# Attention over two key blocks at a time: both score products, then the values of the two blocks before, across pair and group borders, with two sum banks

## The chip, the core and the metric

The kernel runs on one core of a Trainium2 chip. The metric is the device time in microseconds of one execution. The core has TensorE (PE, the matrix engine, which writes to PSUM only), VectorE (DVE), ScalarE (ACT), GpSimd (POOL) and SyncE (SP, which here issues the DMAs of images and results). Each engine works through its own list of instructions in order and waits for other engines by semaphores. PSUM has eight banks.

## The reference, cut to what matters

The input is four images of 384 channels on a 48 x 48 grid, 2304 tokens each, float32. Eight heads of 48 channels:

```
local  = batchnorm(depthwise 7x7 conv of x)                  # per channel
q,k,v  = layernorm(x) @ qkv_w.T + qkv_b                      # per token
q      = q + layernorm(local)
attn   = softmax(q @ k.T / sqrt(48));  out = attn @ v        # per head, 2304 x 2304
result = x + out @ proj_w.T + proj_b
```

## The kernel before

Everything is in `attention_pass`, called once with `shifted=False`; a second call under a condition (with maxima subtracted) doesn't run on these inputs. An image's 2304 queries are cut into 6 groups (g) of 384, the heads into 4 pairs (p), and the keys into 18 blocks (kb) of 128. For each image, group and pair, `attention` goes over the 18 key blocks:

- **scores** (L435): for both heads of the pair, 48 rows each at partitions 0 and 64, keys times queries into a PSUM tile `s` of two banks (pool `ps_s`, two such tiles, four banks in all);
- **exponentials** (L443): one ScalarE instruction over both heads, into `pt`;
- **values** (L421): `pt` of the block before times its values, with a column of ones that sums the weights, added up over the 18 blocks in one PSUM bank `o` (pool `ps_o`, one bank). The two heads take partitions 0 to 48 and 64 to 112.

After the last block ScalarE (L454) and VectorE (L455) copy the two halves of `o` to `osb`, and the next pair may use the bank.

All other work is cut into small steps by Python generators in a queue `behind`; `advance(units)` runs three steps after each key block, `finish` all that are left. The steps are:

- `kv_part(b, g)`: normalize the tokens, project keys and values;
- `q_part(b, g)`: the 49 taps of the convolution for each of three channel blocks (L265, L269, VectorE, into one buffer `acc`), its transposes to tokens and normalization (`lt`), the normalization of the tokens themselves, and per pair a projection (L206), a transpose of `lt` (L287) and the sum of both (L292), which is the query;
- `pair_output` (L342 to L354): three transposes of `osb` on TensorE, then the division on VectorE into `ao`;
- `group_output` (L368 to L385): three transposes of `ao` to a PSUM bank each, copied to `aoT`, then the output projection (L378), the residual sum (L385), and the DMA out.

`normalized` (L142) turns three blocks of tokens by transposes (L152), copies them out (ACT, L153), takes mean and variance (DVE, L156 and L157), raises to -1/2 on GpSimd (L159, L160) and normalizes (DVE, L164); `x_normalized` turns the result back (L190, L193). All these, the projections and the output use one PSUM pool, `ps_m`, of three banks with the tag `m`.

The query work of group g + 1 is queued at pair 0 of group g; before pair 3 `finish` runs what is left of it. A pair's output is appended at the queue's end after its last block.

The order on each engine isn't that of the source: the tile framework schedules when the program is built and moves instructions of independent work past each other on each engine, within what the buffers allow. So steps such as the taps, which need no PSUM, are moved far ahead.

## Time and profile before

| | us |
|---|---|
| median of 3 runs (4406.0 to 4411.12) | 4408.76 |
| the profiled execution | 4405.68 |
| its span, from the first to the last instruction | 4403.8 |
| ACT busy on exponentials (L443) | 1388.8 |
| DVE busy on taps (L269) | 1870.4 |
| PE rows of the scores (L435) | 1725.5 |
| PE rows of the values (L421) | 1510.4 |

A row of the profile names a line, an engine, an operation and its tiles; "x4" is the number of instructions merged into it. In a timeline the first figure is the start within the span, the second the time from the first instruction's start to the last one's end, and a bracket at the end holds the idle time ahead and who ended it. PE's rows overlap a little, since a matmul's end is modelled: starts are the safer figures. The clock is the share of TensorE's full speed that was granted. Here are the slices of the whole span, in tenths:

```profile
PE   6899999999899989999989999999998999999998
DVE  7674835735634484484372547546528174664510
ACT  2344343444334434434433443443443344344444
PEclk9889988999899989999989998999998999899999
```

PE is busy nearly everywhere, with dips at the same place in each image; DVE's share swings between the stretches with taps and those without.

### The profile page before, as it was taken

Reading aid. Unit: us, or ns where it says so; the run is one execution under the profiler, and the core shown is the slowest. Engines: PE = TensorE matmul, PEld = TensorE weight load, DVE = VectorE, ACT = ScalarE, POOL = GpSimd, SP = SyncE. Lnnn points to the kernel's source line nnn. Section 1 sums busy time; section 2 is a strip of 40 time slices with the busy share of each in tenths; the row PEclk is TensorE's granted clock in tenths of the full one; section 3 lists DMA queues with packets and bytes.
Section 4 is the critical chain, followed back from the end, with each engine's and each line's share of the span. In section 5 each row is a group of like instructions: output and inputs, shape, how many; then the busy total and the mean of one; then the engine's idle time right before and its main releaser. Section 6 shows DMA issues by size and latency. Waiting matters only on the chain.

```text
span 4403.8 us, 45704 instructions
## 1 busy us (share of the span) xinstructions
PE 4059.2 (92%) x17714; PEld 1551.7 (35%) x17714; DVE 2339.0 (53%) x4908; ACT 1760.3 (40%) x2449; POOL 182.1 (4%) x325
## 2 busy tenths in 40 slices
PE   6899999999899989999989999999998999999998
PEld 3433332333353333333344333333334433233332
DVE  7674835735634484484372547546528174664510
ACT  2344343444334434434433443443443344344444
POOL 1000000000000000000000000000000000000000
PEclk9889988999899989999989998999998999899999
DMA  2000000000000000000000000000000000000000
GB/s 57 0 1 6 6 1 6 6 33 6 6 1 1 6 6 1 6 6 33 6 6 1 1 6 6 1 6 6 36 2 6 1 6 1 6 6 1 6 6 7
DMA packets 20420, 33.99 MB, mean 8 GB/s; under 512 B 8416, under 2 KB 18656, under 8 KB 18656
## 3 DMA queue, kind: packets, MB, share of 16 engines
q1 hardware_dynamic: 12096, 28.32, 1.7%
q10 hardware_dynamic: 8096, 2.65, 0.3%
q8 instruction: 141, 2.31, 0.2%
q14 instruction: 87, 0.71, 0.1%
HBM read 16.80 MB, written 14.16 MB: 7 GB/s over the span
## 4 chain that ended last, share of the span: by engine, by line
PE 65%; DVE 29%; POOL 3%; ACT 2%; issue 1%; DMA 0%; ACTq 0%; POOLq 0%
DVE acc L269 23%; PE s L435 23%; PE o L421 21%; PE pm L206 10%; PE pm L378 3%; PE pm L228 3%; PE pm L190 2%; DVE st L156 2%; POOL rs L160 1%; PE pm L368 1%; PE pm L152 1%; ACT pt L443 1%; DVE osb L455 1%; PE pm L287 1%; DVE lt L164 1%
## 5 line engine op out<-in xcount | busy, mean ns | idle before, releaser
L443 ACT ACTIVATE pt<-s 128x768 f32<-128x768 f32 x1728 | 1388.8, 810 | 1546.4 <-PE s L435 1505.7
L269 DVE SCALAR_TENSOR_TENSOR acc<-x,cw,acc 128x368 f32<-128x368 f32 (+10 forms) x3456 | 1870.4, 588 | 36.5
L435 PE MATMUL s<-q,k 48*128 48x384 f32 x6912 | 1725.5, 546 | 5.7 <-ACT pt L443 5.7
L421 PE MATMUL o<-pt,v 128*49 128x384 f32 x6912 | 1510.4, 517 | 49.7 <-DVE osb L455 36.3
L435 PEld LDWEIGHTS s<-q,k 48*128 48x128 f32 x6912 | 583.0, 189 | 1070.6 <-issue 1018.2
L421 PEld LDWEIGHTS o<-pt,v 128*49 128x49 f32 x6912 | 310.1, 124 | 984.3 <-issue 887.6
L455 DVE COPY osb<-o 49x384 f32<-49x384 f32 x96 | 53.8, 560 | 939.0 <-ACT osb L454 937.5
L206 PE MATMUL pm<-xnT,w_qk 128*128 128x384 f32 x1152 | 454.0, 546 | 2.9 <-ACT xnT L193 2.9
L156 DVE BATCH_NORM_STATS2 st<-xt 128x6 f32<-128x384 f32 x216 | 112.4, 547 | 609.8 <-ACT xt L153 609.1
L206 PEld LDWEIGHTS pm<-xnT,w_qk 128*128 128x128 f32 x1152 | 236.6, 215 | 182.8 <-issue 41.8
L190 PE MATMUL pm<-ident,xt 128*128 128x128 f32 x432 | 98.5, 381 | 144.0 <-DVE xt L164 142.9
L378 PE MATMUL pm<-aoT,w_o 128*128 128x384 f32 x432 | 170.0, 546 | 0.0
L153 ACT COPY xt<-pm 128x384 f32<-128x384 f32 x216 | 93.2, 484 | 181.9 <-PE pm L152 181.8
L342 PE MATMUL pm<-ident,osb 113*128 113x113 f32 x288 | 54.0, 303 | 119.1 <-DVE osb L455 115.9
L193 ACT ACTIVATE xnT<-pm,ln_sb 128x384 f32<-128x384 f32 x144 | 88.0, 668 | 185.9 <-PE pm L190 185.9
L213 ACT ACTIVATE q<-pm,qkb 128x384 f32<-128x384 f32 x96 | 55.7, 581 | 227.5 <-PE pm L206 227.5
L228 PE MATMUL pm<-w_v,xnT 128*128 128x384 f32 x432 | 144.0, 487 | 0.0
L235 DVE TENSOR_TENSOR v<-pm,vb 128x384 f32<-128x384 f32 x72 | 40.0, 555 | 183.0 <-PE pm L228 183.0
L190 PEld LDWEIGHTS pm<-ident,xt 128*128 128x128 f32 x432 | 70.3, 191 | 185.1 <-DVE xt L164 103.0
L159 POOL TENSOR_SCALAR rs<-mv 128x3 f32<-128x3 f32 x72 | 28.6, 397 | 2569.3 <-DVE mv L157 2569.3
L378 PEld LDWEIGHTS pm<-aoT,w_o 128*128 128x128 f32 x432 | 90.5, 219 | 68.8 <-issue 31.9
L213 ACT ACTIVATE k<-pm,qkb 128x384 f32<-128x384 f32 x96 | 55.7, 580 | 142.0 <-PE pm L206 142.0
(52 smaller groups left out, 1057.0 us busy)
## 6 DMA issues: line engine op xcount, KB each, us to landing
x<-in_x_dram SPq DMA_DIRECT2D x12, 1152.0 KB, 7.5
out_dram<-xr SPq DMA_DIRECT2D x72, 192.0 KB, 1.8
w_qk<-in_qkv_wT_dram ACTq DMA_DIRECT2D x6, 192.0 KB, 5.1
w_v<-in_qkv_wT_dram ACTq DMA_DIRECT2D x3, 192.0 KB, 5.4
w_o<-in_proj_wT_dram ACTq DMA_DIRECT2D x3, 192.0 KB, 3.9
vb<-in_v_b_dram ACTq DMA_DIRECT2D x1, 192.0 KB, 4.4
cw<-in_conv_w_dram ACTq DMA_DIRECT2D x1, 73.5 KB, 5.9
ln_p<-in_ln_pair_dram ACTq DMA_DIRECT2D x2, 1.5 KB, 5.2
```

The lines of the kernel that those rows point to most:

```text
L153: nc.scalar.copy(xt[:, blk, :], tp[:, :C])
L156: nc.vector.bn_stats(st[:, blk, :], xt[:, blk, :])
L190: nc.tensor.transpose(tp[:, blk * P : (blk + 1) * P], kept["xn"][:, blk, c * P : (c + 1) * P], ident)
L206: nc.tensor.matmul(ps[:, :G], lhsT=w_qk[:, c, which, 2 * p : 2 * p + 2, :].rearrange("p h d -> p (h d)"), rhs=xnT[:, c, :], start=c == 0, ...
L213: nc.scalar.activation(dst, ps[:, :G], AF.Identity, bias=qkb[:, which, p : p + 1])
L228: nc.tensor.matmul(ps[:, :C], lhsT=xnT[:, c, blk * P : (blk + 1) * P], rhs=w_v[:, c, :], start=c == 0, stop=c == CC - 1,)
L269: nc.vector.scalar_tensor_tensor(dst, src, cw[:, c, t : t + 1], dst, ALU.mult, ALU.add)
L378: nc.tensor.matmul(ps[:, :G], lhsT=w_o[:, c, co * P : (co + 1) * P], rhs=aoT[:, c, :], start=c == 0, stop=c == CC - 1,)
L421: nc.tensor.matmul(o[r : r + HA, :G], lhsT=values[b, kb // NB][:, kb % NB, 2 * p + j, :], rhs=pt[:, j, :], start=kb == 0, stop=kb == KB - 1,)
L435: nc.tensor.matmul(s[:, j, :G], lhsT=keys[b, kb // NB][r : r + HS, p, blk * P : (blk + 1) * P], rhs=q[r : r + HS, :], start=True, stop=True,)
L443: nc.scalar.activation(pt, s[:, :, :G], AF.Exp, scale=SCALE)
L455: nc.vector.tensor_copy(osb[64 : 64 + HA, :], o[64 : 64 + HA, :G])
```

## The change

Blocks are handled in batches of `BATCH = 2`. A batch issues both score products and both exponentials, and then the values of the batch before, also when that belongs to the pair before or to the group before: the closure that does it is kept in the list `weighing`. The copies of the sums to `osb` follow the last values of a pair, wherever these come, and the pair's division is handed on in `divisions`, to be put at the head of the queue `behind` at the next batch, ahead of the taps. The sums get two banks and the other work two in place of three; `pt` gets four buffers in place of three; the six steps of two blocks run at once after a batch. `finish` moves, for this pass, from pair 3 to pair 0. At the end of an image the last values, divisions and output are issued before the key and value parts of the next.

```diff
-    ps_o = ctx.enter_context(tc.tile_pool(name="ps_o", bufs=1, ...PSUM))
-    ps_m = ctx.enter_context(tc.tile_pool(name="ps_m", bufs=3, ...PSUM))
+    ps_o = ctx.enter_context(tc.tile_pool(name="ps_o", bufs=2, ...PSUM))
+    ps_m = ctx.enter_context(tc.tile_pool(name="ps_m", bufs=2, ...PSUM))
...
+    weighing = []
+    divisions = deque()
+    def weigh_last():
+        if weighing:
+            weighing.pop()()
...
+        def weigh(batch):
+            for kb, pt in batch:
+                for j in range(2):
+                    r = 64 * j
+                    nc.tensor.matmul(o[r : r + HA, :G], ...)
+            if batch[-1][0] == KB - 1:
+                nc.scalar.copy(osb[0:HA, :], o[0:HA, :G])
+                nc.vector.tensor_copy(osb[64 : 64 + HA, :], o[64 : 64 + HA, :G])
+                divisions.append((b, g, p, osb))
+        for k0 in range(0, KB, BATCH):
+            while divisions:
+                done = divisions.popleft()
+                if done[2] == NP - 1:
+                    behind.appendleft(group_output(*done[:2]))
+                behind.appendleft(pair_output(*done))
+            batch = []
+            for kb in range(k0, k0 + BATCH):
...
+                pt = work.tile([P, 2, G], F32, tag="pt", name="pt", bufs=2 * BATCH)
+                nc.scalar.activation(pt, s[:, :, :G], AF.Exp, scale=SCALE)
+                batch.append((kb, pt))
+            weigh_last()
+            weighing.append(lambda batch=batch: weigh(batch))
...
+            advance(BATCH * units)
...
-                if p == NP - 1 and g < NG - 1:
+                if p == (NP - 1 if shifted else 0):
                     finish()
...
+        weigh_last()
+        while divisions:
+            behind.append(pair_output(*divisions.popleft()))
+        behind.append(group_output(b, NG - 1))
```

How the built program's order moves is shown at three places, all in the first image. The lines of the changed kernel are 1 to 20 higher. Names: `q_2_3` is the query tile of group 2, pair 3; `k_5` and `v_5` are keys and values of group 5; "x2" counts matmuls of one head each.

**TensorE, the border from group 2, pair 3 to group 3, pair 0.** Before:

```order
L421 MATMUL o<-pt,v_4_526 49x384 x2
L435 MATMUL s<-q_2_3_2440,k_5_609 128x384 x2
L421 MATMUL o<-pt,v_5_610 49x384 x2
L435 MATMUL s<-q_2_3_2440,k_5_609 128x384 x2
L421 MATMUL o<-pt,v_5_610 49x384 x2
L435 MATMUL s<-q_3_0_3274,k_0_189 128x384
L421 MATMUL o<-pt,v_5_610 49x384 x2
L435 MATMUL s<-q_3_0_3274,k_0_189 128x384 x3
L342 MATMUL pm<-ident,osb 128x113 x3
L368 MATMUL pm<-ident,ao 128x128 x6
```

Now:

```order
L455 MATMUL s<-q_2_3_2537,k_5_609 128x384 x4
L431 MATMUL o<-pt,v_4_526 49x384 x2
L431 MATMUL o<-pt,v_5_610 49x384 x2
L455 MATMUL s<-q_3_0_3357,k_0_189 128x384 x4
L431 MATMUL o<-pt,v_5_610 49x384 x4
L455 MATMUL s<-q_3_0_3357,k_0_189 128x384 x2
L455 MATMUL s<-q_3_0_3357,k_1_273 128x384 x2
L431 MATMUL o<-pt,v_0_190 49x384 x4
L343 MATMUL pm<-ident,osb 128x113 x3
L369 MATMUL pm<-ident,ao 128x128 x3
L455 MATMUL s<-q_3_0_3357,k_1_273 128x384
L369 MATMUL pm<-ident,ao 128x128 x3
```

Scores and values now stand in runs of four where they alternated in runs of two, the last values of the old pair stand behind the first scores of the new one, and the transposes of `osb` come after one more batch.

**TensorE, the normalization of the next tokens around pair 3 of group 2** (`x_83` is the image, `xt` its turned and normalized tokens). Before:

```order
L152 MATMUL pm<-ident,x_83 128x128 x2
L421 MATMUL o<-pt,v_5_610 49x384 x2
L152 MATMUL pm<-ident,x_83 128x128 x7
L435 MATMUL s<-q_2_3_2440,k_0_189 128x384 x6
L190 MATMUL pm<-ident,xt 128x128 x9
L435 MATMUL s<-q_2_3_2440,k_1_273 128x384
```

Now:

```order
L343 MATMUL pm<-ident,osb 128x113 x3
L153 MATMUL pm<-ident,x_83 128x128 x3
L455 MATMUL s<-q_2_3_2537,k_1_273 128x384
L153 MATMUL pm<-ident,x_83 128x128 x3
L455 MATMUL s<-q_2_3_2537,k_1_273 128x384 x3
L431 MATMUL o<-pt,v_0_190 49x384 x2
L431 MATMUL o<-pt,v_1_274 49x384 x2
L191 MATMUL pm<-ident,xt 128x128 x2
L455 MATMUL s<-q_2_3_2537,k_2_357 128x384
L191 MATMUL pm<-ident,xt 128x128
L455 MATMUL s<-q_2_3_2537,k_2_357 128x384 x3
L431 MATMUL o<-pt,v_1_274 49x384 x4
```

Between the last transpose in and the first one out stood three score blocks; now there stand one and a half score blocks and two value blocks, and the transposes of `osb` come just ahead.

**VectorE, the copy of the sums at the border from group 2 to group 3** (`acc` is written by a tap, `ao` by the division). Before, with 58 taps ahead of the copy back to the last of a division:

```order
L269 SCALAR_TENSOR_TENSOR acc<-x_83,cw,acc 128x8x47 x2
L455 COPY osb<-o 49x384
L269 SCALAR_TENSOR_TENSOR acc<-x_83,cw,acc 128x384
L269 SCALAR_TENSOR_TENSOR acc<-x_83,cw,acc 128x8x46
L348 RECIPROCAL rden<-pm 128x6
L269 SCALAR_TENSOR_TENSOR acc<-x_83,cw,acc 128x8x47
L353 SCALAR_TENSOR_TENSOR inside<-rden,inside 128x6
L354 TENSOR_TENSOR ao<-pm,rden 128x3x96
```

Now, with 37 taps ahead of it back to the last query:

```order
L270 SCALAR_TENSOR_TENSOR acc<-x_83,cw,acc 128x384
L440 COPY osb<-o 49x384
L270 SCALAR_TENSOR_TENSOR acc<-x_83,cw,acc 128x8x47
L270 SCALAR_TENSOR_TENSOR acc<-x_83,cw,acc 128x8x46 x2
L270 SCALAR_TENSOR_TENSOR acc<-x_83,cw,acc 128x8x45 x3
L349 RECIPROCAL rden<-pm 128x6
L270 SCALAR_TENSOR_TENSOR acc<-x_83,cw,acc 128x8x46
L354 SCALAR_TENSOR_TENSOR inside<-rden,inside 128x6
L355 TENSOR_TENSOR ao<-pm,rden 128x3x96
```

The copy still stands behind a long run of taps, a shorter one, and six taps in place of two lie between it and the division.

More of the change, by code (lines that the diff above doesn't have):

```diff
@@ L20 @@
 BN_EPS = 1e-5
+BATCH = 2
 RG = 8
@@ new lines, in attention @@
+        for k0 in range(0, KB, BATCH):
[6 more added lines that the diff above has]
+            for kb in range(k0, k0 + BATCH):
+                s = ps_s.tile([P, 2, 512], F32, tag="s", name="s")
+                blk = kb % NB
+                for j in range(2):
+                    r = 64 * j
+                    nc.tensor.matmul(
+                        s[:, j, :G],
+                        lhsT=keys[b, kb // NB][r : r + HS, p, blk * P : (blk + 1) * P],
+                        rhs=q[r : r + HS, :],
+                        start=True,
+                        stop=True,
+                    )
+                pt = work.tile([P, 2, G], F32, tag="pt", name="pt", bufs=2 * BATCH)
[3 more added lines that the diff above has]
+            weighing.append(lambda batch=batch: weigh(batch))
+            for _ in range(BATCH):
+                if ahead is not None:
+                    next(ahead, None)
+            advance(BATCH * units)
```

48 lines of the change are left out of this document (9 added, 39 removed).

## The prediction

> **What bounds the kernel now.** I read the page's table of busy shares first, then who TensorE (PE) waited for, then its timeline row by row, then its clock.
>
> ```profile
> PE 4059.2 (92%) x17714; PEld 1551.7 (35%) x17714; DVE 2339.0 (53%) x4908; ACT 1760.3 (40%) x2449; POOL 182.1 (4%) x325
> core 0: 4403.8 us, clock 0.935
> PE pm L190 <- DVE xt L164: 142.9, 48, 13.5
> PE pm L342 <- DVE osb L455: 115.9, 27, 5.7
> PE o L421 <- DVE osb L455: 36.3, 12, 6.6
> ```
>
> PE is the bound: it idles 4403.8 - 4059.2 = 345 us in all, and VectorE (DVE) and ScalarE (ACT) have half their time free. The last three rows give total, count and longest of PE's waits for DVE: 295 of those 345 us. The second row is the granted clock of 0.935: 6.5% of the span, 286 us, is lost to a halved clock. So time comes back from three places: work on PE itself, the waits, and the slow stretches.
>
> PE's own work first. A float32 matmul stands as two instructions, so one key block is four rows of scores (L435, two heads side by side) and four of values (L421); a smaller count is a missing record. First column start, second duration:
>
> ```profile
> 606.19 0.85 PE L421 MATMUL o<-pt,v 128*49 128x384 f32 x4
> 606.98 0.92 PE L435 MATMUL s<-q,k 48*128 48x384 f32 x4
> 607.82 0.85 PE L421 MATMUL o<-pt,v 128*49 128x384 f32 x4
> ...
> 471.19 1.55 PE L435 MATMUL s<-q,k 48*128 48x384 f32 x6
> 472.67 0.51 PE L342 MATMUL pm<-ident,osb 113*128 113x113 f32 x3
> 473.11 2.79 PE L421 MATMUL o<-pt,v 128*49 128x384 f32 x16
> 475.83 0.92 PE L435 MATMUL s<-q,k 48*128 48x384 f32 x4
> ...
> 636.86 2.10 PE L206 MATMUL pm<-xnT,w_qk 128*128 128x384 f32 x6
> 638.80 0.49 PE L287 MATMUL pm<-ident,lt 128*128 128x128 f32 x3
> 639.12 2.10 PE L206 MATMUL pm<-xnT,w_qk 128*128 128x384 f32 x6
> ```
>
> The reader is to compare starts. Alternating, the values of a block take 606.98 - 606.19 = 0.79 us and its scores 607.82 - 606.98 = 0.84: 1.63 per block. At a pair's border two score blocks stand together and take 472.67 - 471.19 = 1.48, so the second costs 0.64; four value blocks take 475.83 - 473.11 = 2.72, so each after the first costs (2.72 - 0.79)/3 = 0.643. Six rows of a full matmul take 1.94, that is 0.647 for two: 0.64 is the bare work, and the rest is paid where the kind of matmul changes: **0.20 from scores to values, 0.14 back**.
>
> The waits and what follows them:
>
> ```profile
> 505.32 0.82 PE L342 MATMUL pm<-ident,osb 113*128 113x113 f32 x3 [5.13 <-DVE osb L455]
> 551.64 0.85 PE L421 MATMUL o<-pt,v 128*49 128x384 f32 x4 [3.28 <-DVE osb L455]
> 626.01 2.53 PE L190 MATMUL pm<-ident,xt 128*128 128x128 f32 x9 [3.11 <-DVE xt L164]
> ...
> 500.00:520.00 20.00, 14.87 (x41) 7.51 (x41) 15.32 (x34) 3.39 (x6) 0.41 (x1) 0.74 0.05 20
> 548.00:570.00 22.00, 18.72 (x54) 4.62 (x52) 3.32 (x6) 6.13 (x8) 0.00 (x0) 0.61 0.00 0
> 1811.00:1833.00 22.00, 18.72 (x86) 5.30 (x82) 3.93 (x7) 8.90 (x12) 0.00 (x0) 0.92 0.00 1
> 622.00:642.00 20.00, 16.75 (x55) 9.67 (x55) 15.10 (x33) 5.72 (x9) 1.75 (x3) 0.74 0.00 1
> 795.00:815.00 20.00, 16.75 (x62) 9.87 (x59) 15.74 (x36) 5.67 (x10) 2.61 (x5) 0.83 0.00 0
> ```
>
> Three stalls in one group of queries: for the copied sums before their transposes, for the one sum bank, for the normalized tokens. The third figure from the end of a window row is the granted clock. A stall of 3 us or more is followed by a halved clock that costs (1 - 0.74) x 20 = 5.2 us after the first kind, (1 - 0.61) x 22 = 8.6 or (1 - 0.92) x 22 = 1.8 after the second, 5.2 or 3.4 after the third.
>
> **The change, part by part** (sums against the profiled execution: 4405.68 us, span 4403.8).
>
> *Batches of two.* Counted over PE's order of instructions in the pass that runs, changes from scores to values fall from 1586 to 851 and back from 1532 to 613; changes to or from full matmuls (projections, transposes) rise from 555 to 923. Saved 735 x 0.20 + 919 x 0.14 = 276 us. A change to a full matmul costs 1.48 - 2 x 0.64 = 0.20 by the row at 471.19, and one back 0.44 - 0.33 = 0.11 (472.67 to 473.11, three transposes being the 0.32 of 638.80 to 639.12). I take 0.125 x 368 = 46 lost (37 to 74). Score blocks split in two, whose heads no longer run side by side, go from 258 to 274 halves: 16 x 0.32 = 5 lost. **225 us gained** (195 to 235).
>
> *ACT stays hidden.*
>
> ```profile
> L443 ACT ACTIVATE pt<-s 128x768 f32<-128x768 f32 x1728 | 1388.8, 810 | 1546.4 <-PE s L435 1505.7
> ...
> 621.12 1.51 ACT L443 ACTIVATE pt<-s 128x768 f32<-128x768 f32 x2 [0.33 <-PE s L435]
> ```
>
> A batch is 1.48 + 0.79 + 0.64 = 2.91 us on PE; its two exponentials take 1.51 on ACT, 0.33 after the first scores. They end about 0.9 + 0.33 + 1.51 = 2.7 us after the batch began, and the second one's bank is wanted at 2.91 + 0.64 = 3.55. Nothing waits; were those 0.8 us of cover gone, each batch would be late by what is missing. Four `pt` buffers suffice: a batch's values stand ahead of the next batch but one.
>
> *Two sum banks* remove the third wait row wholly: 36.3 us, in eight stalls of 3.28, one of 6.55 and three of 1.18. Clock after them: five windows of 0.60 or 0.61 (8.6 each), three of 0.92 (1.8), and
>
> ```profile
> 216.00:240.00 24.00, 17.45 (x51) 4.46 (x52) 23.23 (x42) 5.30 (x7) 0.00 (x0) 0.57 0.00 1
> 1150.00:1172.00 22.00, 20.67 (x109) 6.77 (x109) 21.67 (x49) 10.66 (x14) 1.81 (x7) 1.00 0.00 1
> ```
>
> 10.3 after the longest and none after the short ones. 36 + 43 + 5 + 10 = **95 us gained**. What is late next there: the pair's transposes, which now come one batch after its last values.
>
> *Those transposes at a group's border* wait for the copy that stands on DVE behind taps of the convolution.
>
> ```profile
> 468.73 0.61 DVE L292 SCALAR_TENSOR_TENSOR q<-pm,ln_p,q 128x384 f32<-128x384 f32 x1
> 469.26 1.62 DVE L269 SCALAR_TENSOR_TENSOR acc<-x,cw,acc 128x368 f32<-128x368 f32 x3
> ...
> 474.72 29.95 DVE L269 SCALAR_TENSOR_TENSOR acc<-x,cw,acc 128x368 f32<-128x368 f32 x58
> 504.70 0.56 DVE L455 COPY osb<-o 49x384 f32<-49x384 f32 x1
> ...
> 515.16 0.62 DVE L385 SCALAR_TENSOR_TENSOR xr<-pm,pb,xr 128x384 f32<-128x384 f32 x1 [4.59 <-PE pm L378]
> ```
>
> A tap takes 29.95/58 = 0.516 us, and 58 of them made the 5.13 us wait. Now 37 stand between the group's last query and the copy. I start both engines at the end of the second query's transpose. DVE: 0.15 of delay, three queries of 0.53, 9 + 5 + 37 taps, the copy: 0.15 + 1.6 + 26.3 + 0.6 = 28.7 us. PE, up to the transposes: two units of projection and transpose (1.94 + 0.32 each), half a score block (0.84), the rest of two split batches (2.3 and 2.95), five whole batches of 2.91: 25.2 us. Wait 3.5; in the first and last group, counted in the same way, 4.1 and 4.6. That is about 1.2 less than now at 20 borders, **24 us gained**; the halved clock behind it stays. At the next border 38 taps, the copy and one addition (19.6 + 0.6 + 0.6) run against eight batches, 23.3 us: some 2.5 us of cover. At the other two borders no tap stands ahead of the copy, or two.
>
> *Normalized tokens.*
>
> ```profile
> 619.19 0.98 PE L152 MATMUL pm<-ident,x 128*128 128x128 f32 x7
> 623.72 0.17 DVE L157 BATCH_NORM_AGGREGATE mv<-st 128x2 f32<-128x6 f32 x1
> 625.47 1.26 DVE L164 TENSOR_SCALAR xt<-xt,mv,rs 128x384 f32<-128x384 f32 x3 [1.09 <-POOL rs L160]
> ...
> 1137.70 2.33 PE L190 MATMUL pm<-ident,xt 128*128 128x128 f32 x9 [6.55 <-DVE xt L164]
> ...
> 1134.00:1154.00 20.00, 14.97 (x59) 9.33 (x61) 17.76 (x44) 4.83 (x9) 2.48 (x5) 0.83 0.00 0
> ```
>
> Today 626.01 - 620.1 = 5.9 us pass from the last transpose in to the first one out, 626.01 - 623.89 = 2.1 of them after the last variance. In the new order a pair's copy, five taps and its division are queued on DVE inside this chain. From the third transpose of the convolution on, DVE reaches that copy's end after 6.3 us (3.4 to the local normalization, 1.3 for it, two taps, the copy), the division's after 11.2, the last variance after 12.9, and the tokens are out at 15.0. PE has a split batch, a whole one, four transposes, half a score block and a split batch: 2.95 + 2.91 + 4 x 0.33 + 0.84 + 2.95, about 10.9. Wait 4.1 for 3.11, at 16 places: **15 us lost**. At the three borders to a new image the wait of 6.55 meets two batches, 5.9 us: gone, with 3.4 of clock each, **30 gained**.
>
> *One bank fewer for the rest.* Of three transposes to one tile each, the third now waits until the first is copied out.
>
> ```profile
> L153 ACT COPY xt<-pm 128x384 f32<-128x384 f32 x216 | 93.2, 484 | 181.9 <-PE pm L152 181.8
> ```
>
> 0.48 + 0.2 of delay less the second unit's 0.33: 0 to 0.7 us at 144 places, 0 to 100 us. Inside the loop scores lie between these units; I take 0.5 at the 42 places of the 21 key/value parts run in a lump: **20 lost**.
>
> *At nothing:* `finish`, moved to p = 0, finds a queue that pair 3 has emptied. SP issues its DMAs in the same order. On POOL the fill of the next `osb` now stands between a group's two inverse roots and waits for a pair's transposes; these end 6 us ahead of the second root's variance (6.4 against 12.9 above), and if they didn't, the chain would be later by the rest. The load of the next image waits for transposes that now end some 43 us ahead of its first reader, and three loads of 7.5 us take at most 23.
>
> ```profile
> x<-in_x_dram SPq DMA_DIRECT2D x12, 1152.0 KB, 7.5
> ```
>
> Sum: 225 + 95 + 24 + 30 - 15 - 20 = **339 us**. 4405.7 - 339 = 4067; the median shown is 3.1 above the profiled execution: **4070 us**.
>
> **The rivals.** *Slower: each border stalls.* If DVE's taps ran late at every border, the transposes, placed one batch after the values, would stall PE like the one at the group's border: 3.9 us and 5.2 of clock, 9.1, at up to 72 more borders: 4070 + 655 = 4725. It decides from 339/9.1 on, 38 of the 72. For it: the waits of 5.13 and 3.28 were both for such a copy, and today the transposes of three pairs of four come much later. Against: in DVE's new order two of these three borders have no run of taps ahead. With the remaining one alone stalling (24 x 9.1 = 218) it would be 4290, still faster.
>
> *The second block of a batch is no cheaper*: its weights use the same rows of the array, so their load could be exposed.
>
> ```profile
> L435 PEld LDWEIGHTS s<-q,k 48*128 48x128 f32 x6912 | 583.0, 189 | 1070.6 <-issue 1018.2
> ```
>
> One load of 0.19 us would eat the 0.20 of a change. Then only 339 - 225 of the gain is left, and the 51 us of new changes and halves are still paid: 4406 - 114 + 51 + 3 = 4346. Against it: the 1.48 and 2.72 us above. The Trainium skill has it as a rule (TensorE: Matmul & The Clock Gate, "Part 3: Packing small matmuls"): a weight load overlaps running matmuls only when its row group differs. By that rule the batch would gain nothing and the sum would be this rival's; the trace disagrees, its second block cost 0.64.
>
> *The clock comes back sooner.* With 1.8 us lost after a stall, as in three of eight windows, in place of 4.4 to 5.2, the 43 stalls left would cost 130 us less: 3940. The Trainium skill (same page, "Part 1: The HAM clock gate") says that about 3.4 us of sustained work restore the clock. By that the loss is 1.7 us each time and the time again about 3940; the 0.92 row agrees, the 0.74 and 0.61 rows don't.
>
> That the change doesn't do what it says is excluded: the new order shows 722 runs of four score matmuls, where 1445 runs of two stood.
>
> **How the numbers follow.** Forecast (3980 to 4200, from the stalls' 1.5 us either way, the clock and the bank's 0 to 100): 0.68. Clock sooner 0.13, one border stalling 0.07, no cheaper block 0.04, slower 0.05, some balance near no change 0.03. Range 3920 to 4230 leaves out 0.19. About 0.2% is what a measurement of this kernel can tell from no change: faster 0.92, same 0.03, slower 0.05.
>
> **What would show it.** Right: scores and values in runs of eight rows, 1.48 and 1.43 us apart; no PE wait of L431 for `osb`; waits of 3 to 5 us before the transposes at group borders and of about 4 before the normalized ones; a clock near 0.94 to 0.95. Wrong: runs of eight that take 1.6 us, waits at the borders inside a group, PE waits for ACT at L153 or L191, or a third kind of stall.

## The result and the profile after

The changed kernel took **4068.56 us** (median of 4 runs, 4068.25 to 4069.32), the kernel before 4408.26 beside it (4406.0 to 4411.12): the ratio is 0.9229, 95% interval 0.9213 to 0.9245. The forecast was 4070. The profiled execution took 4069.32 us. The page's busy shares after, and then the span with its clock:

```profile
PE 3792.6 (93%) x17714; PEld 1655.5 (41%) x17714; DVE 2347.7 (58%) x4908; ACT 1695.6 (42%) x2449; POOL 189.5 (5%) x325
```

```profile
core 0: 4067.5 us, clock 0.947
```

PE idles 4067.5 - 3792.6 = 275 us, where it idled 345. The clock takes (1 - 0.947) x 4067.5 = 216, where it took 286. What is left of PE's busy time without that, its **work** from here on, is 3792.6 - 216 = 3577, where it was 4059.2 - 286 = 3773. So the 336 us between the two profiled executions are 196 of work, 70 of idle time and 70 of clock. PE's waits after, total, count and longest:

```profile
PE pm L343 <- DVE osb L440: 105.9, 34, 8.1
PE pm L191 <- DVE xt L165: 99.9, 54, 6.0
PE pm L369 <- DVE ao L355: 15.1, 9, 3.8
```

The values (now L431) wait for no copy of sums any more. The reader is to see that the transposes of the copied sums wait nearly as long in all as before (115.9), and more often: 34 times for 27. PE's timeline after, one group's stalls and between them a steady batch:

```profile
604.35 0.71 PE L191 MATMUL pm<-ident,xt 128*128 128x128 f32 x2 [3.41 <-DVE xt L165]
...
630.58 1.56 PE L455 MATMUL s<-q,k 48*128 48x384 f32 x8
632.07 1.50 PE L431 MATMUL o<-pt,v 128*49 128x384 f32 x8
633.50 1.56 PE L455 MATMUL s<-q,k 48*128 48x384 f32 x8
...
648.60 0.51 PE L343 MATMUL pm<-ident,osb 113*128 113x113 f32 x3 [3.35 <-DVE osb L440]
...
690.30 0.51 PE L343 MATMUL pm<-ident,osb 113*128 113x113 f32 x3 [3.38 <-DVE osb L440]
```

A batch takes 633.50 - 630.58 = 2.92 us (2.91 was forecast). The stalls at 604 and 648 are the two that were forecast, 4.1 and 3.5 there. The one at 690 is at the second border of the group, where the prediction saw 2.5 us of cover. The clock in windows around them (the third figure from the end):

```profile
624.00:644.00 20.00, 20.00 (x103) 8.40 (x103) 20.00 (x40) 9.92 (x15) 0.42 (x1) 1.00 0.00 1
644.00:664.00 20.00, 16.65 (x58) 7.85 (x56) 18.56 (x38) 3.81 (x7) 0.41 (x1) 0.83 0.05 20
...
684.00:704.00 20.00, 16.62 (x76) 6.49 (x75) 6.73 (x14) 6.86 (x10) 0.41 (x1) 0.83 0.00 1
...
1688.00:1708.00 20.00, 18.04 (x91) 7.08 (x91) 2.60 (x8) 8.00 (x11) 0.41 (x1) 0.91 0.00 1
```

A stall followed by 0.83 costs (1 - 0.83) x 20 = 3.4 us of clock besides its own length; the last row, the same stall at the second border in another image, costs 1.8. Four of the eight stalls at second borders are followed by 0.83 and four by 0.91, 21 us in all. The clock records of the two whole traces say more than windows do: the granted clock is 1 or 0.5 and nothing between, and the stretches at half clock are nearly all multiples of 3.41 us. Before there were 64 of them (27 of 6.8 us, 24 of 10.2, six of 17 or 20, the rest shorter), after 59 (38 of 6.8, 12 of 10.2, two of 13.7, the rest shorter). So the 70 us of clock came from shorter stretches more than from fewer.

### The profile page after: what moved, and what is told of

The parts are those of the page before. It is cut to its first block, busy times and chain, and to the rows that moved or that the text cites. A ratio compares the mean times of both kernels' runs of the same rounds, so it can differ in the third digit from the quotient of the medians.

```text
span 4067.5 us, 45598 instructions
## 1 busy us (share of the span) xinstructions
PE 3792.6 (93%) x17714; PEld 1655.5 (41%) x17714; DVE 2347.7 (58%) x4908; ACT 1695.6 (42%) x2449; POOL 189.5 (5%) x325
## 4 chain that ended last, share of the span: by engine, by line
PE 61%; DVE 34%; POOL 2%; issue 1%; ACT 1%; DMA 0%; ACTq 0%; POOLq 0%; DVEq 0%
DVE acc L270 27%; PE s L455 24%; PE o L431 20%; PE pm L207 7%; PE pm L379 3%; PE pm L229 2%; DVE st L157 2%; PE pm L191 2%; POOL rs L161 1%; DVE xt L165 1%; PE pm L153 1%; DVE q L293 1%; PE pm L343 1%; PE pm L369 1%; DVE osb L440 1%
## 5 line engine op out<-in xcount | busy, mean ns | idle before, releaser
L463 ACT ACTIVATE pt<-s 128x768 f32<-128x768 f32 x1728 | 1316.1, 808 | 1307.2 <-PE s L455 1306.8
L455 PE MATMUL s<-q,k 48*128 48x384 f32 x6912 | 1551.1, 526 | 1.2 <-ACT pt L463 1.2
L431 PE MATMUL o<-pt,v 128*49 128x384 f32 x6912 | 1330.6, 505 | 0.0
L455 PEld LDWEIGHTS s<-q,k 48*128 48x128 f32 x6912 | 648.8, 190 | 697.3 <-ACT pt L463 364.7
L431 PEld LDWEIGHTS o<-pt,v 128*49 128x49 f32 x6912 | 381.8, 125 | 825.5 <-issue 823.3
L207 PE MATMUL pm<-xnT,w_qk 128*128 128x384 f32 x1152 | 424.8, 517 | 0.3 <-ACT q L214 0.3
L207 PEld LDWEIGHTS pm<-xnT,w_qk 128*128 128x128 f32 x1152 | 219.7, 200 | 183.3 <-issue 24.8
L191 PE MATMUL pm<-ident,xt 128*128 128x128 f32 x432 | 103.4, 354 | 107.2 <-DVE xt L165 99.9
L379 PE MATMUL pm<-aoT,w_o 128*128 128x384 f32 x432 | 182.1, 578 | 0.0
L343 PE MATMUL pm<-ident,osb 113*128 113x113 f32 x288 | 51.1, 288 | 105.9 <-DVE osb L440 105.9
L191 PEld LDWEIGHTS pm<-ident,xt 128*128 128x128 f32 x432 | 60.5, 168 | 194.2 <-issue 75.7
L425 POOL MEMSET osb<- 32x384 f32 x96 | 39.9, 416 | 1802.1 <-PE pm L343 1648.7
```

The source lines that it names most:

```text
L191: nc.tensor.transpose(tp[:, blk * P : (blk + 1) * P], kept["xn"][:, blk, c * P : (c + 1) * P], ident)
L207: nc.tensor.matmul(ps[:, :G], lhsT=w_qk[:, c, which, 2 * p : 2 * p + 2, :].rearrange("p h d -> p (h d)"), rhs=xnT[:, c, :], start=c == 0, ...
L379: nc.tensor.matmul(ps[:, :G], lhsT=w_o[:, c, co * P : (co + 1) * P], rhs=aoT[:, c, :], start=c == 0, stop=c == CC - 1,)
L431: nc.tensor.matmul(o[r : r + HA, :G], lhsT=values[b, kb // NB][:, kb % NB, 2 * p + j, :], rhs=pt[:, j, :], start=kb == 0, stop=kb == KB - 1,)
L455: nc.tensor.matmul(s[:, j, :G], lhsT=keys[b, kb // NB][r : r + HS, p, blk * P : (blk + 1) * P], rhs=q[r : r + HS, :], start=True, stop=True,)
L463: nc.scalar.activation(pt, s[:, :, :G], AF.Exp, scale=SCALE)
```

## The experiments

Theory: the time is PE's work, set by the changes of the kind of matmul, plus its stalls on VectorE (DVE) with their clock. Rivals: the gain is in the sum banks or in the borders; or DVE sets the pace, so that what PE saves comes back as a wait. Line numbers in their rows are within a few of those of the changed kernel, or of the kernel before where the edit starts from that.

All runs in one table, us. Idle time, clock and work are worked out from each profiled execution as above (the clock is given to a thousandth, which is 4 us). "Count" is what the prediction's prices (0.20, 0.14, 0.125 and 0.32 us) make of the changes in that kernel's order of instructions.

| kernel | median | ratio, interval | idle | clock | work | count |
|---|---|---|---|---|---|---|
| before | 4408.3 | | 345 | 286 | 3773 | 684 |
| the change | 4068.6 | 0.9229 (0.9213-0.9245) | 275 | 216 | 3577 | 459 |
| batches inside a pair only | 4093.7 | 0.9287 (0.9264-0.9309) | 415 | 262 | 3417 | 344 |
| before, two other banks | 4421.5 | 1.0031 (1.0016-1.0046) | 305 | 230 | 3883 | 730 |
| before, two sum banks and two others | 4347.3 | 0.9864 (0.9844-0.9883) | 223 | 152 | 3969 | 794 |
| the change, batch of one | 4229.6 | 0.9597 (0.9574-0.9621) | 215 | 135 | 3863 | 739 |
| the change, one sum bank, three others | 4026.4 | 0.9135 (0.9113-0.9158) | 371 | 229 | 3423 | 355 |
| the change, both copies on ACT | 3976.2 | 0.9014 (0.8999-0.9029) | 257 | 163 | 3555 | 449 |
| the change, division later | 4064.7 | 0.9216 (0.9201-0.9232) | 332 | 215 | 3511 | 433 |
| the change, taps by turns | 4034.4 | 0.9147 (0.9131-0.9162) | 248 | 210 | 3575 | 459 |
| the change, batch of three | 4147.8 | 0.9402 (0.9387-0.9418) | 399 | 137 | 3610 | 350 |
| one sum bank, copies on ACT | 3930.5 | 0.8921 (0.8896-0.8945) | 338 | 189 | 3404 | 345 |
| the same, taps by turns | 3925.2 | 0.8898 (0.8883-0.8913) | 333 | 177 | 3417 | 353 |
| one sum bank, copies on ACT, output later | 3772.9 | 0.8556 (0.8542-0.8571) | 209 | 117 | 3445 | 340 |

### The batch by itself

```diff
-        for kb in range(KB):
+        for k0 in range(0, KB, 2):
+            batch = []
+            for kb in range(k0, k0 + 2):
...
+                batch.append((kb, pt))
...
-                weigh(*last)
-            last = (kb, pt)
-            advance(units)
+                for item in last:
+                    weigh(*item)
+            last = batch
+            advance(2 * units)
```

(`pt` has four buffers here too; banks, borders and the places of the outputs are those of the kernel before.)

> The kernel before, with batches of two key blocks inside a pair alone: at each pair's end the last values follow as they did, one sum bank and three banks for other work stay, and the copied sums are transposed where they were. By the order of PE's instructions there are 731 changes from scores to values, 696 back, 498 to or from full matmuls and 118 split halves of a score block, which the prediction's prices make 344 us where the kernel before has 684. Theory (the gain is the changes of the kind of matmul): 340 us less than before at most, about 4070 us, so as fast as the change itself; if the stalls move a little, 4040 to 4110. Rival (the gain came from the two banks or from the borders): 4340 us or more. Rows: score batches and value batches start 1.49 and 1.43 us apart inside a pair; PE's waits for the copied sums stay near 36 us at the values and 116 us at the transposes.

It took 4093.65 us, 315 less than before: within the theory's 4040 to 4110, far from the rival's 4340. PE's work fell by 3773 - 3417 = 356 for the 340 of the count. But PE waits more; its waits:

```profile
PE pm L342 <- DVE osb L460: 152.7, 23, 7.9
...
PE o L421 <- DVE osb L460: 61.3, 13, 8.3
```

They were 115.9 and 36.3, and the expectation that they stay so failed. The likely reason is that PE comes to the same copies sooner; no run separates that from the changed order. The batch alone brings 93% of the change's gain.

### The banks by themselves

```diff
# two other banks
-    ps_m = ctx.enter_context(tc.tile_pool(name="ps_m", bufs=3, ...PSUM))
+    ps_m = ctx.enter_context(tc.tile_pool(name="ps_m", bufs=2, ...PSUM))
# and with two sum banks
-    ps_o = ctx.enter_context(tc.tile_pool(name="ps_o", bufs=1, ...PSUM))
+    ps_o = ctx.enter_context(tc.tile_pool(name="ps_o", bufs=2, ...PSUM))
```

> The kernel before, with two banks in place of three for all matmuls but scores and values; nothing else. It is the price of the bank that the change gives up. The prediction's term: 20 us (0 to 100), so 4410 to 4510, most likely 4430. A second count, by the order of instructions: the planner then places work otherwise and the changes to full matmuls rise from 555 to 770, which by the prediction's prices makes 46 us more, so 4450 or, with the term, 4470. Rival (the bank costs nothing, since other work stands in the way between uses): 4400 to 4415.

> The kernel before with two sum banks and two other banks, nothing else; the run with two other banks and one sum bank (4421 us) is its counterpart. It prices the second sum bank by itself: the prediction's term is 36 us of waits and 59 of halved clock. By the order of instructions the changes of kind cost 794 us where that counterpart has 730. Theory (the second bank takes away the 32 us of waits of the values for the copied sums, and their clock): PE's idle time and halved clock together fall by 60 to 100 from the counterpart's 305 and 230, its work rises by some 64, and the time is 4390 to 4430, as good as no gain. Rival (the stall only moves to the sums' transposes): the waits for the copied sums stay at 110 us in all, and the time is 4460 to 4490.

Taking a bank from the other work cost 13 us (4421.48): inside the term's range, less than the 46 of the second count, a little more than the rival's. The parts are larger than their sum: work rose by 110, idle time and clock fell by 40 + 56. The waits of the kernel with two other banks:

```profile
PE pm L190 <- DVE xt L164: 107.2, 49, 6.0
PE pm L342 <- DVE osb L455: 83.5, 31, 4.6
PE o L421 <- DVE osb L455: 32.0, 28, 5.9
```

The source of DVE's work wasn't changed, and yet PE waits less for it: most likely a slower PE comes later to the same stall. With two sum banks beside that:

```profile
PE pm L190 <- DVE xt L164: 85.2, 41, 6.0
PE pm L342 <- DVE osb L455: 71.9, 24, 3.9
```

The values' wait for the copied sums is gone, idle time and clock fall by 82 + 78 = 160 against the kernel with two others, work rises by 86, and the time falls by 74 (4347.29), outside both forecasts. Together with the order that comes with it, the second sum bank takes away more stalls than the 95 us that the prediction gave it, and costs more work. Only 32 of the 82 us of idle time are the values' own wait; 22 went at the tokens and 12 at the copied sums.

### The borders and banks without the batch

```diff
-BATCH = 2
+BATCH = 1
```

> The change with batches of one block: scores of one key block, then the values of the preceding one, over pair and group borders, with two sum banks and two other banks. Only the batch is undone. 1703 changes from scores to values, 1402 back, 962 to or from full matmuls: by the prediction's prices 739 us, 55 more than before, while two sum banks, group borders, image borders, tokens and the other bank give back 95 + 24 + 30 - 15 - 20 = 114. Theory (the batch carries the gain, the second bank and the borders some of it): 4350 us, 4300 to 4400. Rival (the borders and the banks carry it, the batch little): 4120 us or less. A second rival (the banks and borders are worth nothing by themselves): 4460.

4229.55 us lies between theory and rival, 179 below the kernel before. The profiled execution was this kernel's fastest, 4215.37, so the parts in the table are those of a time 14 us lower. Work rose by 3863 - 3773 = 90, of which the count says 55. Idle time and clock fell by 130 + 151. So the new places of the values and outputs and the second bank are worth much where PE is slow. From here to the change the batch saves 3863 - 3577 = 286 us of work, for 280 by the count, but only 146 of time between the profiled executions (161 between the medians): idle time rises by 60 and clock by 81.

### One sum bank

```diff
-    ps_o = ctx.enter_context(tc.tile_pool(name="ps_o", bufs=2, ...PSUM))
-    ps_m = ctx.enter_context(tc.tile_pool(name="ps_m", bufs=2, ...PSUM))
+    ps_o = ctx.enter_context(tc.tile_pool(name="ps_o", bufs=1, ...PSUM))
+    ps_m = ctx.enter_context(tc.tile_pool(name="ps_m", bufs=3, ...PSUM))
```

> The change with one sum bank and three banks for other work, as in the kernel before; the batches of two and their run over the borders stay. The changes of kind fall with the bank: 848, 610 and 660 to or from full matmuls, 56 split halves, 355 us by the prediction's prices where the change has 459. Theory (the second sum bank is worth the 95 us that the prediction gave it): the waits of the values for the copied sums come back and the time is about 4060 (4068 - 104 + 95), between 4030 and 4170. Rival (two score blocks of the next batch and the moved transposes cover the copy, so that the second bank is worth little and the third other bank more): 3950 to 4000 us, faster than the change.

4026.35 us, 42 below the change, between the rival's 4000 and the theory's 4030. The waits came back, as the theory had it, and are six times those of the kernel before:

```profile
PE o L431 <- DVE osb L440: 216.0, 47, 10.5
```

but work fell by 3577 - 3423 = 154 against 109 more of idle time and clock. One place of it, DVE's rows:

```profile
617.62 20.15 DVE L270 SCALAR_TENSOR_TENSOR acc<-x,cw,acc 128x368 f32<-128x368 f32 x39
637.80 0.56 DVE L440 COPY osb<-o 49x384 f32<-49x384 f32 x1
638.39 3.15 DVE L270 SCALAR_TENSOR_TENSOR acc<-x,cw,acc 128x376 f32<-128x376 f32 x6
```

The copy of half a microsecond stands behind 39 taps; PE waits 6.51 us for it, up to 638.41.

### Both copies on ScalarE

```diff
-                nc.vector.tensor_copy(osb[64 : 64 + HA, :], o[64 : 64 + HA, :G])
+                nc.scalar.copy(osb[64 : 64 + HA, :], o[64 : 64 + HA, :G])
```

> The change with the second copy of a pair's sums on ACT too, where the first already is, so that neither stands behind DVE's taps. Theory (the stalls ahead of the copied sums' transposes are the copy's place in DVE's queue): the 106 us of PE's waits for that copy fall below 25 us; the two stalls of 3.4 us in each group go with the halved clock behind them (3.4 us each). Eight places at the second border and about 18 at the group's last border at 3.4 + 3.4 would make 170 us, so 3900; what the next wait on DVE (the pair's division, which still stands behind the taps) takes in their place is bounded by the 106 us and their clock. I expect 4015, between 3900 and 4070. Rival (the taps themselves set the time, so the wait only moves to the division or the normalized tokens): 4050 to 4070, with 80 us or more of new waits of the output transposes for the divided sums.

3976.17 us, 92 below the change. The 106 us of waits for the copied sums are gone wholly, and most of their length stands now at the next wait:

```profile
PE pm L191 <- DVE xt L165: 102.9, 64, 6.0
PE pm L369 <- DVE ao L355: 100.0, 19, 6.5
```

So idle time fell by 18 us only; 53 came from the clock (19 waits for the division where 34 stood for the copy) and 22 from work. Theory and rival both hold in part.

### The division later

```diff
-            while divisions:
+            while divisions and k0 >= 4 * BATCH:
```

> The change with the transposes of a pair's copied sums, and what follows them, taken from the fifth batch of the next pair at the earliest, where the change takes them after the first: some 8 to 9 us later. Theory (the transposes stand too close behind the copy; DVE needs 2 to 5 us more): the 106 us of waits for the copied sums and about 70 us of halved clock behind them vanish, and the changes of kind cost 26 us less by their count: 3870 to 3920. Rival (DVE is late by as much for what comes next, the divided sums, the tokens): the waits turn into waits for these, and the time is 4030 or more.

4064.73 us against 4068.56: the rival. The waits for the copied sums fell from 105.9 to 5.6 us, and

```profile
PE pm L369 <- DVE ao L355: 143.5, 19, 10.2
PE pm L191 <- DVE xt L165: 132.3, 62, 6.0
```

took their place. The division has to pass the same run of taps, and the output's transposes follow it at once. Work fell by 66 us (26 by the count), and idle time rose by 57.

### The taps by turns

```diff
-        for c in range(CC):
-            img = xs[:, c, :].rearrange("p (h w) -> p h w", w=W)
-            a = acc[:, c, :].rearrange("p (h w) -> p h w", w=W)
-            for t in taps:
+        for t in taps:
+            for c in range(CC):
+                img = xs[:, c, :].rearrange("p (h w) -> p h w", w=W)
+                a = acc[:, c, :].rearrange("p (h w) -> p h w", w=W)
```

> The change with the convolution's taps in another order: each tap for all three channel blocks in turn, where the change does all taps of one block, then the next. The sums and their order within a block are the same. Theory (a tap that adds to the sums that the tap just ahead wrote takes 0.66 us, and one whose sums were written two taps ahead 0.52): every tap takes about 0.52, DVE's taps take some 100 us less in all, the eight stalls of 3.4 us at a group's second border vanish with their clock, and the time is 4010 to 4020. Rival (0.66 us has another cause, as the shape of the rows or ACT and PE beside it): the slow taps stay at 0.6 us or more in some stretch, and the time is 4060 to 4075.

4034.40 us, 34 below the change: the cause is the theory's, the size less than it said. The timeline of the changed kernel, with a copy on GpSimd (POOL) that falls into such a run, and then the taps ahead of the copies at a group's first and second border:

```profile
510.89 25.04 DVE L270 SCALAR_TENSOR_TENSOR acc<-x,cw,acc 128x384 f32<-128x384 f32 x38
...
512.98 1.44 POOL L251 COPY xr<-x 128x1152 f32<-128x1152 f32 x1 [17.86 <-DMA out_dram<-xr]
...
628.82 19.12 DVE L270 SCALAR_TENSOR_TENSOR acc<-x,cw,acc 128x360 f32<-128x360 f32 x37
...
664.61 25.04 DVE L270 SCALAR_TENSOR_TENSOR acc<-x,cw,acc 128x384 f32<-128x384 f32 x38
```

The run at the first border (628.82) takes 19.12/37 = 0.517 us a tap, those at the second 25.04/38 = 0.659. By turns, at the second border:

```profile
506.62 19.18 DVE L270 SCALAR_TENSOR_TENSOR acc<-x,cw,acc 128x368 f32<-128x368 f32 x37
...
508.70 18.09 POOL L251 COPY xr<-x 128x1152 f32<-128x1152 f32 x1 [17.59 <-DMA out_dram<-xr]
```

0.518 us. What a tap itself takes, with the smallest, the middle and the largest in ns, is nearly the same in the two runs at the second border:

```profile
L270 DVE SCALAR_TENSOR_TENSOR acc<-x,cw,acc x38: 593/603/1364, 664.6 to 689.1; 128x376 f32<-128x376 f32 x11, 128x368 f32<-128x368 f32 x11, 128x360 f32<-128x360 f32 x11, 128x384 f32<-128x384 f32 x5
...
L270 DVE SCALAR_TENSOR_TENSOR acc<-x,cw,acc x37: 583/598/614, 506.6 to 525.2; 128x376 f32<-128x376 f32 x12, 128x368 f32<-128x368 f32 x10, 128x360 f32<-128x360 f32 x9, 128x384 f32<-128x384 f32 x6
```

The difference is when the next one starts: by turns before the one ahead has ended, 0.50 to 0.53 us after its start; with the taps of one block in a row 0.036 us after its end, 0.63 to 0.65 after its start. And one tap of the 38, the one that meets GpSimd's copy, takes 1.364. Only the order of the taps is another: now each follows two taps on other channel blocks, where in the run of 25.04 us all 38 followed one another on one block, as their widths in the order of instructions show (48, 47, 46, 45, 45, 46, 47, 48 columns, once each; in the run of 37 two such rows are interleaved). So a tap right behind one on the same sums costs 0.13 us more, 4.8 over 38, and the tap that is held up another 0.76. The eight stalls of 3.38 there are gone, and PE's idle time falls by just that, 27 us. In the first image the stretch between two first borders takes 148.0 us (489.76 to 637.79) for 154.8 (493.76 to 648.60), 6.8 less: the stall and its 3.4 of clock. Over the eight stalls, four of them with 1.8 of clock, that would be 27 + 21 = 48; 34 came. The clock records show where the rest went: the 12 waits for the tokens in an image's groups between its first and its last are now 3.82 us for 3.41, and the stretches at half clock that meet them add up to 143 us in place of 102, so 20 us more are lost there. Why a wait 0.4 us longer costs that much clock, no run here shows.

### Batches of three

```diff
-BATCH = 2
+BATCH = 3
```

> The change with batches of three key blocks in place of two; two tiles of scores as before, two sum banks, two others. By the order of instructions 562 changes from scores to values, 375 back, 854 to or from full matmuls, 246 halves: 350 us by the prediction's prices, 109 less than the change. Theory (every change of kind avoided is gained while ACT hides): 3960. Rival (the third score block's tile is free only when the first exponential has ended, some 0.33 + 0.75 us after the first scores' end, when PE has issued the second block for 0.64 us): PE waits about 0.5 us for ACT in each of 576 batches, no clock lost, +290 against -109: about 4250; with half of that wait, 4100.

4147.77 us, 79 above the change: the theory's 3960 is refuted, and the time lies between the rival's 4100 and 4250. PE's timeline:

```profile
639.78 1.56 PE L455 MATMUL s<-q,k 48*128 48x384 f32 x8
641.66 0.92 PE L455 MATMUL s<-q,k 48*128 48x384 f32 x4 [0.33 <-ACT pt L463]
642.51 2.14 PE L431 MATMUL o<-pt,v 128*49 128x384 f32 x12
644.58 1.56 PE L455 MATMUL s<-q,k 48*128 48x384 f32 x8
```

The third scores wait for the first exponential, as the rival had it, 0.33 us in 526 places, 172 us in all. A batch takes 4.80 us, where six blocks at 0.64 and one change each way make 4.18: the wait of 0.33 costs 0.62. The row counts the first eight as 1.56 long, where the next four would have started after 1.28; that is the other 0.28. This is ACT's cover of 0.8 us, which the prediction counted for batches of two, used up.

### One sum bank with both copies on ScalarE, and two steps further

The edits of "one sum bank" and "both copies on ScalarE" together; then, apart, the taps by turns, or this:

```diff
+    outputs_due = deque()
...
                 if done[2] == NP - 1:
-                    behind.appendleft(group_output(*done[:2]))
+                    outputs_due.append(done[:2])
                 behind.appendleft(pair_output(*done))
+            while outputs_due and k0 >= 4 * BATCH:
+                behind.appendleft(group_output(*outputs_due.popleft()))
```

> The change with one sum bank and three other banks (as in the run with one sum bank, 4026 us) and both copies of the sums on ACT (as in the run with the copies on ACT, 3976). Theory (the 216 us of waits of the values for the one bank were the copy's place behind DVE's taps, so they go with it, and the bank is better used for other work): 345 us of changes, PE's work as in the run with one sum bank less 10 (3413), idle and halved clock as in the run with the copies on ACT (257 and 163): 3833, or 3860 as faster work on PE meets the divided sums a little earlier. Rival (DVE sets the time, and whatever PE saves comes back as waits): 3940 to 3980, with more than 150 us of waits for the divided sums and 120 for the tokens.

> One sum bank, three other banks, both copies on ACT, and the convolution's taps by turns over the three channel blocks. Theory (the 34 us that turns brought to the change were its stalls of the copy at a group's second border, which are gone here already): the same time as without turns, within 10 us. Rival (shorter taps shorten every wait on DVE): 30 us or more below it.

> One sum bank, three other banks, both copies on ACT, and the group's output (transposes of the divided sums, projection) taken from the fifth batch of the next group's first pair, where the change takes it right behind the last pair's transposes. Theory (the 19 stalls of 4 to 5 us for the divided sums, 100 us with the copies on ACT, are only a place chosen too early): they go with the halved clock behind them, 3.4 us each, so some 130 to 160 us less than without it: about 3710. Rival (the waits go to the tokens): within 30 us of the time without it.

Together the first two took 3930.47 us: 70 above the theory, 10 below the rival's range. Work was 3404, as the theory had it, the 216 us of waits for the bank are gone, and its waits are those that the rival named:

```profile
PE pm L369 <- DVE ao L355: 159.2, 22, 10.0
PE pm L191 <- DVE xt L165: 145.3, 50, 12.8
```

Taps by turns gave 3925.21, 5 less, as the theory had it: shorter taps alone don't help where the copies are no longer behind them. With the output later it is **3772.89 us**, 158 below the version without, as much as forecast as a difference (130 to 160; the 3710 started from a time 60 to 90 us too low). It is 0.8556 of the kernel before (0.8542 to 0.8571), and 3772.89/4068.56 = 0.927 of the changed kernel. Its waits:

```profile
PE pm L191 <- DVE xt L165: 162.8, 53, 12.0
...
PE pm L369 <- DVE ao L355: 6.0, 7, 1.8
```

and its timeline, where the stall for the divided sums was 7.32 us in the version without:

```profile
592.94 1.50 PE L432 MATMUL o<-pt,v 128*49 128x384 f32 x8
594.37 1.20 PE L369 MATMUL pm<-ident,ao 128*128 128x128 f32 x9
595.49 6.07 PE L379 MATMUL pm<-aoT,w_o 128*128 128x384 f32 x18
```

Of 159 us of waits 153 are gone, and 17 came back at the tokens; clock lost is 117 for 189, and work rose by 41, which the count doesn't show. So DVE doesn't set the pace over a group; a few places do where PE asks for something a little too early.

## Why the prediction held, step by step

**Changes of kind: right.** Work fell by 196 where 225 was forecast. The table shows the price list at work in the other kernels. Work less count is 3059 to 3105 in the six with three banks for other work (mean 3076), and 3078 to 3175 in the seven with two, batches of three left out (mean 3124); batches of three, with their 526 waits, have 3260. So one list of four prices holds within some 50 us over kernels whose counts run from 340 to 794. "The second block is no cheaper" is excluded: batches start 2.92 us apart. The Trainium skill's rule on weight loads (TensorE: Matmul & The Clock Gate, "Part 3: Packing small matmuls") would have made that more; no run here agrees with it.

**One bank fewer: 20 us, as waits.** Waits for copies on ACT ahead of transposes hardly show: 9.2 us at L153, of which 8.1 is one wait at the start, and 5.5 at L191. The two means of work differ by 48 us, but that isn't the bank alone. The count leaves out value blocks split in two, of which PE's order in the traces has 18 before, 84 with two other banks and 188 with two sum banks beside them; each half takes 0.78 us, as long as a whole block, so at 0.32 that is up to 54 us more. It also takes 0.125 us for a change from scores to a full matmul that takes 0.20 (half a score block between full matmuls takes 0.84). With these two put in, the means differ by 27. No run prices the bank apart from the order that comes with it.

**Two sum banks, 95 us: the stalls right in kind, the balance wrong.** The 36 us of waits went, as said, and in the kernel before, with its own order, the second bank takes 160 of idle time and clock. But the bank comes from the other work, and the prediction spread the price of that over two other terms: 263 of its 368 new changes to and from full matmuls (923, against 660 with one sum bank) belong to the swap. By its own prices, 104 of count and 20 for the bank against 95, the swap inside the change loses 29 us. Measured, it loses 42. Beside the batch the second bank is a loss; in the kernel before it was a gain of 61 (4408.3 to 4347.3).

**Transposes of the copied sums: the step that failed.** "At the next border 38 taps, the copy and one addition (19.6 + 0.6 + 0.6) run against eight batches, 23.3 us: some 2.5 us of cover". The taps take 25.04 us there, 5.4 more, and PE stalls for 3.38 in eight of 24 groups (at the others fewer taps stand there): 27 us of idle time and 21 of clock. The stalls at the first border got shorter, 5.13 to 3.35, and at the last group's 4.80 to 3.23. In place of 24 us, 10 were gained. The row that tells it stood in the trace of before, behind another border:

```profile
521.40 29.51 DVE L269 SCALAR_TENSOR_TENSOR acc<-x,cw,acc 128x384 f32<-128x384 f32 x45
```

29.51/45 is 0.656, one tap of 1.354 beside GpSimd's copy included. One price was taken from the first run of taps and used for another run that has one channel block left. It is the rival "one border stalls" at a third of its places and at 6.0 us for 9.1, and the "third kind of stall" that the prediction named as a sign against itself.

**Normalized tokens: mis-sized to the other side.** 4.1 for 3.11 was forecast, 3.41 came, at 12 places; in each image's first group the wait fell from 4.52 to 2.99 and in its last from 2.33 to 0.34. The three waits of 6.55 are gone, and 2.71 to 2.75 stand near there in their place. The row fell from 142.9 to 99.9, where 5 us had been forecast (30 less 10 of its clock, less 15). Some 8 of these 43 only moved: the very first wait, 13.53 before, is 3.92 now, with 8.09 for a copy on ACT ahead of it. The rest makes up for most of the eight stalls above.

**Clock: the sum right, by another way.** 69 us were forecast (59 behind the sum bank's stalls, 10 at the image borders) and 70 came, although eight new stalls cost 21. Most stalls now cost 3.4 us, and not the 4.4 to 5.2 of the forecast. "The clock comes back sooner" wanted 1.8 us; that came at four of the eight new stalls, and in six of the 59 stretches in all. The Trainium skill's rule (same page, "Part 1: The HAM clock gate") has the clock back after about 3.4 us of work. The trace agrees in those six; in 38 stretches half clock lasts twice that, and in 14 longer still (part of some of them falls into the stall itself).

**The parts don't add up.** The batch alone gives 315 us, and 161 on top of the rest; the rest alone gives 179, and 25 on top of the batch. A faster PE meets the same copies, divisions and tokens earlier. The prediction recomputed the waits for the new pace in each place, so its total didn't count this gain twice. That it came within 2 us is also luck. By kind of loss the forecast was 225 of work, 45 of idle time (36 + 24 + 20 - 15 - 20) and 69 of clock; 196, 70 and 70 came. 29 too little of work and 25 more of idle time cancel. Within the idle time the row of the copied sums gave 14 less than forecast and that of the tokens 38 more, and a new wait of 15.1 for the divided sums (L369) stands in no term.

## What to carry to other kernels

Time saved on the engine that bounds a kernel comes back in part at each place where it waits for another, so recompute each wait at the new pace, and after the change look for the consumer that was placed a few microseconds too early: moving one of them gave 158 us here, in a kernel with one sum bank and both copies on ACT, while moving another (the division) gave nothing. When two pools share the banks, price the swap as one thing, with the changes in the instruction order that it brings. Take the price of a run of like instructions from that run, not from its neighbour: what stands just ahead on the same data may make each one dearer.

## What the runs showed of the hardware

- A DVE instruction that adds to the sums written by the one just ahead starts 0.63 to 0.65 us after it, 0.036 after its end; if taps on other channel blocks stand between, it starts 0.50 to 0.53 us after the one ahead, before that has ended (128 x 360 to 128 x 384, float32, sums in SBUF). What each takes is about 0.60 us in both.
- In the run of dependent taps GpSimd's copy of 128 x 1152 takes 1.44 us, and one tap beside it 1.364 in place of 0.60. Among taps by turns the same copy takes 18.09 and ends, at 526.79, about a microsecond after the run's last tap (525.80); over all 24 copies the median is 1.43 us in the changed kernel and 13.38 by turns. So GpSimd gets through between dependent taps and not between taps that overlap. The Trainium skill says that a DVE instruction with two SBUF inputs contends with a GpSimd instruction that reads SBUF (SBUF — State Buffer, "Who interferes with whom"). The trace agrees, and shows that the rest of a run of 37 instructions can hold the copy off.
- The granted clock is 1 or 0.5 in these traces, and nearly all stretches at 0.5 are multiples of 3.41 us: behind stalls of about 3.4 us they lasted 3.4, 6.8 or 10.2.
- A wait of 0.33 us between two pairs of matmuls cost 0.62, in batches of three.
